# Layer 2 of a four-layer recurrent kernel: where the second sequence's queries, keys and values are projected

## The chip, the cores and the metric

The kernel runs on one core of one Trainium2 chip. The metric is the device time of one execution in microseconds (us); lower is better. One launch computes the whole model. The engines are TensorE (PE; its weight loads are shown as PEld), VectorE (DVE), ScalarE (ACT), GpSimd (POOL) and SyncE (SP, which issues DMAs). Each takes its own instructions in order and waits for the others by semaphores.

## The reference, cut to what matters

The model has four layers over 2 sequences of 1024 tokens with 128 channels. Each layer computes `x = x + s * silu(f)`, where `s` is a sequence mixer and `f` a feed-forward block, both from the layer-normed `x`. In layer 2 the block `f` begins with a softmax attention with 16 query heads of 8 channels in 4 groups that share keys and values:

```python
xr = rope(rms_norm(x, norm1_w))
Q = (xr @ Wq)      # 16 heads of 8
K = (xr @ Wk)      # 4 groups of 8
V = (xr @ Wv)      # 4 groups of 8
scores = einsum('bghsd,bgtd->bghst', Q, K) / sqrt(8)
attn = softmax(scores + causal_mask)
out = einsum('bghst,bgtd->bghsd', attn, V)
h = x + out.reshape(B, S, 128) @ Wo
```

A mixture of 8 experts (2 per token) follows on `h`, and beside it a linear attention gives `s`. The change concerns `Q`, `K` and `V` of the second sequence only.

## The kernel before

The tokens are 16 tiles of 128, 8 per sequence; four tiles make a group of 512 tokens (`G = 4`). `layer2` first normalises `x` (`Kern.normalise`), and then calls `Attention.prepare` once per sequence. For each group of 512 tokens, `prepare` scales the rows (`xw`, ACT), applies the rotation with six POOL instructions (`xr`, lines 1471 to 1476), and turns the result to channels by tokens (`xrT`: four transposes on PE, an eviction on ACT or DVE by turns). Then it projects: per group one product for the keys (`pk`), four for the queries (`pq`), and four small ones for the values (`pv`). Each fp32 product with 512 columns shows as two matmul instructions.

Keys and queries are evicted by `parts` (lines 1448 and 1449): ACT copies the product to `high`, rounded to fp32r, and DVE combines the product with `high`, so that every 8 channels are held as high and low parts. The values go through one DVE copy (line 1496) into `va`, which two POOL memsets prepare. In the preparation all eight PSUM banks belong to the pool `sn2`.

The attention is `softmax_attention`. Its PE order is written out by hand (`manual_schedule` for PE); the order on the other engines, and on PE outside this part, is made by a planner that runs the program against its own timeline and picks what is ready, earlier program order first. PSUM is divided anew: three banks with the tag `pm` (pool `sm2`), two pairs of banks for scores (`psc`, pool `sc2`), one for the output (`pat`, pool `so2`). The pool `pl` (`l2`) holds tiles of the loop in SBUF.

A step is one (sequence, query tile, key tile). There are 72 of them, sequence 0 first (36). For the softmax, the maxima of every query row are needed before its scores are exponentiated. They come from units: a score product into a `pm` bank (`pm<-kT,qT`; for the diagonal tile after a mask product, `pm<-ngeR,identR`), then a DVE reduction (line 1535) that frees the bank. When all units of a query tile are done, `largest` (lines 1543 to 1548) combines them and `turn` transposes the result (`pmt`, then `mT` on ACT). Four lead-in steps, -4 to -1, do only units, two masked and four plain ones each, so that the first maxima exist when step 0 begins. In steps from 0, PE also computes the scores (`psc`), ACT the exponentials (`pr`, line 291), and PE one step later the products with the values (`pat`).

`fill` is a list of (step, function): the functions are called at the head of the step, ahead of that step's masks, by `run(later.pop(s, ()))`. Before the change the list holds parts of the routing that come after half of the steps. Functions that the attention adds itself (`turn`, and the three parts of `close`) come behind those of `fill` in the same step.

In the lead-in, `take` hands out the units by their due steps:

```python
    for s in range(-4, 0):
        run(later.pop(s, ()))
        phase(take("masked", s, 99))
        phase(take("plain", s, 99))
        finish(s)
```

Of the kernel before, what the change touches and what calls it, by code (L numbers as in the profile page):

```python
# [10 lines left out]
F32 = mybir.dt.float32  # L11
# [8 lines left out]
P = 128  # L20
NB, SEQ = 2, 1024
# [3 lines left out]
G = 4  # L25
# [1057 lines left out]
def layer2(K, x, xn, xT, w, inp):  # L1083
    nc, tc, c = K.nc, K.tc, K.c
    four = [P, G, P]
    flat = lambda a: a.rearrange("p a b -> p (a b)")
    with ExitStack() as es:
# [9 lines left out]
        def norm(gs):  # L1097

            for i in range(gs[0] * G, gs[-1] * G + G):
                K.sumsq(keep, rs[:, i : i + 1], h[:, i, :])  # L1100
            at = slice(gs[0] * G, gs[-1] * G + G)
            K.powers(rs[:, at], rs[:, at], 1.0 / P, 1e-6)
            for g in gs:
                normed[g] = keep.tile(four, F32, name="hn", bufs=2)
                for j in range(G):
                    i = g * G + j
                    nc.vector.scalar_tensor_tensor(normed[g][:, j, :], h[:, i, :], rs[:, i : i + 1], w["n2"], ALU.mult, ALU.mult)
                nc.sync.dma_start(inp["lists"][0].rearrange("(i p) d -> p i d", p=P)[:, g * G : (g + 1) * G, :], normed[g])

        def hidden_columns(g, ps, tag):  # L1110
            pt = ps.tile(four, F32, name="tp", tag=tag)
            for j in range(G):
                nc.tensor.transpose(pt[:, j, :], normed[g][:, j, :], c["ident"])
            K.copy(hT[:, g * G * P : (g + 1) * G * P], flat(pt))

        with ExitStack() as e1:
            pf = e1.enter_context(tc.tile_pool(name="f2", bufs=1))
            K.phase("sqrt_and_others")
            seqs = [Attention(K, pf, xn, w, h, b) for b in range(NB)]
            ms = keep.tile([P, NT], F32, name="ms")  # L1120
            with tc.tile_pool(name="sn2", bufs=8, space=PSUM) as sn, tc.tile_pool(name="p2", bufs=1) as pp:

                n1 = w["n1"].rearrange("p (f two) -> p f two", two=2)
                turn = {}
                for n, a in (("cos", 0), ("sin", 0), ("cos", 1), ("sin", 1)):
                    turn[n, a] = pp.tile([P, TPB, 64], F32, name=f"{n}{a}")
                    nc.gpsimd.tensor_mul(turn[n, a], w[n], n1[:, :, a].unsqueeze(1).to_broadcast([P, TPB, 64]))
                K.normalise(pp, sn, x, xn, xT, None, ms)
                K.rsqrt(r2, ms, 1.0, 1e-5)
                for a in seqs:  # L1130
                    a.prepare(pp, sn, ms, turn)
            for rate, log in inp["rates"]:
                nc.scalar.activation(rate, log, AF.Exp)
            pl = e1.enter_context(tc.tile_pool(name="l2", bufs=1))
            for a in seqs:
                a.loop = pl
            K.phase("natural_log_exp_and_others")
            with tc.manual_schedule(engines={mybir.EngineType.PE}):
                with ExitStack() as e3:
                    sm = e3.enter_context(tc.tile_pool(name="sm2", bufs=3, space=PSUM))  # L1140
                    sc = e3.enter_context(tc.tile_pool(name="sc2", bufs=2, space=PSUM))
                    so = e3.enter_context(tc.tile_pool(name="so2", bufs=1, space=PSUM))

                    half = TPB * (TPB + 1) // 2
                    mid = TPB * (TPB + 1) - G * (G + 1) // 2
                    routed = [(half + 6, lambda: norm([0, 1])), (mid + 6, lambda: norm([3]))]
                    for g, s0 in ((0, half + 9), (1, half + 11), (3, mid + 9)):
                        routed.append((s0, lambda g=g: hidden_columns(g, sm, "pm")))
                        routed.append((s0 + 3, lambda g=g: K.group_logits(sm, "pm", lg, hT, g, w["wr"], w["br"], 8)))
                    softmax_attention(K, pf, sm, sc, so, seqs, routed)  # L1150
        with ExitStack() as e2:
            pa = e2.enter_context(tc.tile_pool(name="a2", bufs=1))
            pf = e2.enter_context(tc.tile_pool(name="m2", bufs=1))
# [6 lines left out]
            with tc.tile_pool(name="r2", bufs=1) as pr:  # L1160
                m1, m2, hot = K.top2(pr, lg, 8)
                d = Dispatch(K, pf, pr, sf, hot, 8, 2 * P, inp["lists"])
# [11 lines left out]
            for n in range(d.n):  # L1174
# [4 lines left out]
                t = pf.tile([P, inp["rows"].shape[2]], F32, name="tw", bufs=3)  # L1179
# [254 lines left out]
class Attention:  # L1434
# [16 lines left out]
    def prepare(self, pp, sc, ms, turn):  # L1451
        K, pf, xn, w, b = self.K, self.pf, self.xn, self.w, self.b
        nc, c = K.nc, K.c
        four = [P, G, P]
        xrT = pp.tile([P, SEQ], F32, name="xrT", bufs=2)
        rs = pp.tile([P, TPB], F32, name="ars", bufs=2)
        for g in range(TPB // G):
            tiles = range(b * TPB + g * G, b * TPB + g * G + G)
            gr = rs[:, g * G : (g + 1) * G]
            K.rsqrt(gr, ms[:, tiles.start : tiles.stop], 1.0, 1e-6)  # L1460
            xw = pp.tile(four, F32, name="xw", bufs=2)
            for j, i in enumerate(tiles):
                nc.scalar.activation(xw[:, j, :], xn[:, i, :], AF.Copy, scale=gr[:, j : j + 1])
            pair = xw.rearrange("p t (f two) -> p t f two", two=2)
            xe, xo = pair[:, :, :, 0], pair[:, :, :, 1]
            at = slice(g * G, g * G + G)
            cose, sine, coso, sino = (turn[n, a][:, at, :] for a in range(2) for n in ("cos", "sin"))
            xr = pp.tile(four, F32, name="xr", bufs=2)
            t2 = pp.tile([P, G, 64], F32, name="t2", bufs=2)
            t3 = pp.tile([P, G, 64], F32, name="t3", bufs=2)  # L1470
            nc.gpsimd.tensor_mul(xr[:, :, :64], xe, cose)
            nc.gpsimd.tensor_mul(t2, xo, sino)
            nc.gpsimd.tensor_sub(xr[:, :, :64], xr[:, :, :64], t2)
            nc.gpsimd.tensor_mul(xr[:, :, 64:], xe, sine)
            nc.gpsimd.tensor_mul(t3, xo, coso)
            nc.gpsimd.tensor_add(xr[:, :, 64:], xr[:, :, 64:], t3)
            K.to_feature_major(sc, lambda i: xr[:, i % G, :], xrT, g)
        self.qT = qT = pf.tile([P, 4, SEQ], F32R, name="qT", bufs=2)
        self.kT = kT = pf.tile([P, SEQ], F32R, name="kT", bufs=2)
        self.va = va = pf.tile([P, TPB, 4, 32], F32, name="va", bufs=2)  # L1480
        nc.gpsimd.memset(va, 0.0)
        nc.gpsimd.memset(va[:, :, :, 8], 1.0)
        for g in range(TPB // G):
            cols = slice(g * 512, (g + 1) * 512)
            pk = sc.tile([P, 512], F32, name="pk", tag="ps")
            K.mm(pk, w["wk"], xrT[:, cols])
            self.parts(pp, kT[:, cols], pk, w["klow"])
            for j in range(4):
                pq = sc.tile([P, 512], F32, name="pq", tag="ps")
                K.mm(pq, w["wq"][:, j, :], xrT[:, cols])  # L1490
                self.parts(pp, qT[:, j, cols], pq, w["qlow"])
            pv = sc.tile([P, G, 32], F32, name="pv", tag="ps")
            for j in range(G):
                i = g * G + j
                K.mm(pv[:, j, :], xrT[:, i * P : (i + 1) * P], w["wv"])
            nc.vector.tensor_copy(va[:, g * G : (g + 1) * G, :, :8], pv.rearrange("p t (g d) -> p t g d", d=8))

    def banks(self, sb):

# [393 lines left out]
def build(tc, io, packs):  # L1893
    nc = tc.nc
    with ExitStack() as ctx:
# [25 lines left out]
        with tc.tile_pool(name="const2", bufs=1) as pool0:  # L1921
            views.update((n, load(pool0, n)) for n in ("l1", "l2"))
            layer1(K, x, xn, xT, views["l1"], {"rows": io["rows1"], "lists": pair, **{n: io[n] for n in ("sw1", "sw3", "sw2")}})
            rates = {d: later.tile([P, 2], F32, name=d + "rate") for d in "fb"}
            layer2(K, x, xn, xT, views["l2"], {"rows": io["rows2"], "lists": pair, "rates": [(rates[d], views["l3"][d + "A_log"]) for d in "fb"]})
# [18 lines left out]
```

## Time and profile before

| | us |
|---|---|
| median of 3 runs | 1352.11 |
| lowest and highest | 1345.19, 1353.02 |
| the profiled execution's own time | 1337.11 |
| span of its trace | 1335.3 |
| PE busy (6697 matmuls) | 1145.4 (86%) |
| DVE busy (2260) | 873.4 (65%) |
| ACT busy (919) | 506.2 (38%) |
| POOL busy (386) | 389.0 (29%) |
| mean granted TensorE clock | 0.905 |

Times in the text are from the start of the span. Layer 2's preparation runs from about 444 to 495.7 us: normalisation and rotation first, sequence 0's projection from 470.6 to 482.8, sequence 1's transposes to 484.0 and its projection from 484.2. The attention follows to about 810 us. The granted clock is the share of full speed that the throttle gave TensorE; it takes the values 0.50 and 1.00, in windows of 3.41 us. "Busy" for PE is from the modelled ends of pipelined matmuls, so a busy PE is not one at its peak. Where a line ends in [time <-engine tile line], it says how long the engine sat idle before it, and what it waited for.

### The profile page before, as it was taken

The page shows a single profiled execution, that of the slowest core. Times are in us where ns is not written, and L with a number is a line of the kernel's source. Part 1 is how long each engine was busy: PE and PEld are TensorE (multiplying, and loading weights), DVE is VectorE, ACT ScalarE, POOL GpSimd, SP SyncE. Part 2 cuts the span into 40 slices and gives each one's busy share as a digit, 9 for nine tenths or more (in the row PEclk, how much of TensorE's full clock was granted, in tenths as well). Part 3 has the DMA queues.
Part 4 walks back from the last instruction along what each step waited for, and adds up shares of the span by engine and source line. Part 5 has one row for each costly group of instructions (what it writes and reads, how often), then busy time and mean ns, then how long its engine had stood idle before and what let it go on. Part 6 is the DMA issues. An engine that isn't in the chain of part 4 may idle for free. (4 is left out here: it accounts for less than half of the span.)

```text
span 1335.3 us, 18604 instructions
## 1 busy us (share of the span) xinstructions
PE 1145.4 (86%) x6697; PEld 773.0 (58%) x6697; DVE 873.4 (65%) x2260; ACT 506.2 (38%) x919; POOL 389.0 (29%) x386
## 2 busy tenths in 40 slices
PE   5599987899998288899999994899999288999996
PEld 2267665888996145454445343677778254554555
DVE  7944368947757965768888537787765582353447
ACT  4633335123222241435555773144243244422221
POOL 0073530057542520000000000344674130634430
PEclk9799986899999585969999997799999668999998
DMA  2000003046352000000000000243445301222101
GB/s 91 1 0 1 1 15 126 4 149 180 117 142 79 0 1 0 1 0 1 1 1 17 1 9 8 97 132 106 125 128 160 109 39 42 41 55 57 47 17 32
DMA packets 37803, 71.26 MB, mean 53 GB/s; under 512 B 5275, under 2 KB 22176, under 8 KB 37328
## 3 DMA queue, kind: packets, MB, share of 16 engines
q1 hardware_dynamic: 31408, 55.09, 13.7%
q0 software_dynamic: 5440, 9.79, 3.0%
q10 hardware_dynamic: 864, 5.20, 1.1%
q8 instruction: 53, 0.87, 0.3%
q14 instruction: 38, 0.31, 0.1%
HBM read 62.58 MB, written 8.85 MB: 53 GB/s over the span
## 5 line engine op out<-in xcount | busy, mean ns | idle before, releaser
L1535 DVE TENSOR_REDUCE mx<-pm 128x1 f32<-128x512 f32 (+3 forms) x304 | 185.4, 656 | 76.5 <-PE pm L319 72.2
L1305 POOL DMA_INDIRECT xb<-xs,dfrom x85 | 84.7, 997 | 491.7 <-PE psum L319 348.3
L291 ACT ACTIVATE pr<-psc 128x1024 f32<-128x1024 f32 x144 | 139.6, 1021 | 101.8 <-PE psc L319 69.5
L319 PE MATMUL pm<-kT,qT 32*128 32x128 f32 (+3 forms) x576 | 110.3, 370 | 7.5 <-DVE mx L1535 6.8
L319 PEld LDWEIGHTS pm<-kT,qT 32*128 32x128 f32 x576 | 68.1, 206 | 78.9 <-DVE mx L1535 52.7
L1315 POOL DMA_INDIRECT ys<-yb,dto x85 | 87.1, 1024 | 80.0 <-DVE yb L1202 49.4
L319 PE MATMUL p<-xbT,tw 128*128 128x256 f32 x368 | 99.8, 387 | 3.7 <-ACT sg L1195 2.6
L319 PE MATMUL pat<-pr,va 128*32 128x512 f32 x576 | 80.8, 633 | 0.9 <-DVE ao L316 0.9
L325 PE MATMUL tp<-w_c,xn 128*128 128x128 f32 x64 | 20.2, 413 | 71.2 <-DVE xn L369 45.1
L1195 ACT ACTIVATE sg<-p,tw 128x256 f32<-128x256 f32 x92 | 41.1, 472 | 90.8 <-PE p L319 86.5
L319 PEld LDWEIGHTS p<-xbT,tw 128*128 128x128 f32 x368 | 63.1, 193 | 14.6 <-ACT sg L1195 4.5
L319 PE MATMUL psc<-qT,kT 32*128 32x512 f32 x288 | 64.3, 492 | 3.8 <-ACT pr L291 3.8
L1196 DVE SCALAR_TENSOR_TENSOR hh<-p,tw,sg 128x256 f32<-128x256 f32 x92 | 42.5, 479 | 32.3 <-ACT sg L1195 23.2
L1874 POOL TENSOR_TENSOR hT<-hT,gb 128x512 f32<-128x512 f32 x32 | 41.3, 1294 | 72.0 <-DVE hT L1872 67.9
L319 PEld LDWEIGHTS po<-tw,hh 128*128 128x128 f32 x368 | 54.7, 193 | 9.4 <-issue 3.6
L1872 DVE TENSOR_TENSOR hT<-hT,put 128x512 f32<-128x512 f32 x36 | 24.5, 685 | 54.5 <-PE put L319 53.1
L325 PEld LDWEIGHTS tp<-w_c,xn 128*128 128x128 f32 x64 | 11.8, 191 | 78.8 <-ACT lnrs L291 45.7
L319 PE MATMUL po<-tw,hh 128*128 128x128 f32 x368 | 56.6, 277 | 0.5 <-DVE hh L1196 0.4
L319 PE MATMUL psc<-mT,onesR 32*128 32x512 f32 x288 | 54.7, 419 | 0.0
L291 ACT ACTIVATE hT<-pgt 128x512 f32<-128x512 f32 x36 | 21.4, 597 | 72.4 <-PE pgt L319 70.0
L605 POOL TENSOR_TENSOR uda<-w_c,vdA 128x512 f32<-128x512 f32 x28 | 28.6, 1041 | 62.1 <-PE pe L319 36.9
L646 DVE TENSOR_TENSOR uxdt<-pt,vdt 128x512 f32<-128x512 f32 x16 | 10.4, 684 | 47.9 <-PE pt L644 47.8
(523 smaller groups left out, 2756.4 us busy)
## 6 DMA issues: line engine op xcount, KB each, us to landing
tw<-in_rows SPq DMA_DIRECT2D x23, 836.0 KB, 4.5
tw<-in_rows SPq DMA_DIRECT2D x39, 384.0 KB, 3.3
gb<-gt SPq DMA_DIRECT2D x32, 256.0 KB, 4.1
yt<-ys SPq DMA_DIRECT2D x16, 256.0 KB, 3.2
w_l<-in_l ACTq DMA_DIRECT2D x1, 1890.0 KB, 11.6
w_e<-in_e SPq DMA_DIRECT2D x1, 1536.0 KB, 8.5
xb<-xs,dfrom POOLq DMA_INDIRECT x85, 2.8
ys<-yb,dto POOLq DMA_INDIRECT x85, 2.3
```

Source lines behind the costliest of these rows:

```text
L291: op = self.nc.scalar.activation(out, in_, func, **kw)
L319: self.nc.tensor.matmul(out, lhsT=lhsT, rhs=rhs, start=start, stop=stop)
L325: self.nc.tensor.transpose(pt[:, j, :], src(g * G + j), self.c["ident"])
L605: pool.tensor_mul(da, upto.unsqueeze(1).unsqueeze(1).to_broadcast(lay), m["dA"][:, i0 + j : i0 + j + per, :].unsqueeze(3).to_broadcast(lay))
L646: nc.vector.tensor_mul(heads(xdt[:, k]), heads(pt), each(m["dt"], k))
L1195: nc.scalar.activation(sg, p1[:, k - k0, :], AF.Silu, bias=t[:, 1536 + k : 1537 + k])
L1196: nc.vector.scalar_tensor_tensor(hh[:, k, :], p2[:, k - k0, :], t[:, 1540 + k : 1541 + k], sg, ALU.add, ALU.mult)
L1305: self.K.nc.gpsimd.indirect_dma_start(dst, None, self.xs, bass.IndirectOffsetOnAxis(self.of_token[:, n : n + 1], 0))
L1315: d = self.K.nc.gpsimd.indirect_dma_start(self.ys, bass.IndirectOffsetOnAxis(self.to[:, n : n + 1], 0), src, None, bounds_check=2 * T - 1, ...
L1535: nc.vector.tensor_reduce(mx[:, starts.index(a), g, j : j + k], tile[0][:, : k * m].rearrange("p (j m) -> p j m", m=m), AX.X, ALU.max)
L1872: nc.vector.tensor_mul(hT, hT, put)
L1874: nc.gpsimd.tensor_mul(hT, hT, gb[k // 2][:, k % 2, :])
```

## The change

`prepare` is cut in two. What is left of it scales, rotates and transposes, and keeps `xrT` in the longer-lived pool `pf`. The new method `project` allocates `qT`, `kT` and `va`, and returns twelve functions: for each of the two groups of 512 tokens one for the keys, four for the queries, one for the values. Sequence 0's are all called in the preparation, now after both sequences were prepared. Sequence 1's are put into the attention's list: numbers 0 to 7 in pairs at the heads of the lead-in steps -4 to -1, numbers 8 to 11 at the heads of steps 0 to 3. There they take their PSUM banks from the three with the tag `pm`, and `high` from the loop's pool.

```diff
--- before.py
+++ after.py
@@ -1129,6 +1129,8 @@
                 K.rsqrt(r2, ms, 1.0, 1e-5)
                 for a in seqs:
                     a.prepare(pp, sn, ms, turn)
+                for part in seqs[0].project(pp, sn, "ps"):
+                    part()
             for rate, log in inp["rates"]:
                 nc.scalar.activation(rate, log, AF.Exp)
             pl = e1.enter_context(tc.tile_pool(name="l2", bufs=1))
@@ -1147,6 +1149,8 @@
                     for g, s0 in ((0, half + 9), (1, half + 11), (3, mid + 9)):
                         routed.append((s0, lambda g=g: hidden_columns(g, sm, "pm")))
                         routed.append((s0 + 3, lambda g=g: K.group_logits(sm, "pm", lg, hT, g, w["wr"], w["br"], 8)))
+                    second = seqs[1].project(pl, sm, "pm")
+                    routed += [(n // 2 - 4 if n < 8 else n - 8, part) for n, part in enumerate(second)]
                     softmax_attention(K, pf, sm, sc, so, seqs, routed)
         with ExitStack() as e2:
             pa = e2.enter_context(tc.tile_pool(name="a2", bufs=1))
@@ -1452,7 +1456,7 @@
         K, pf, xn, w, b = self.K, self.pf, self.xn, self.w, self.b
         nc, c = K.nc, K.c
         four = [P, G, P]
-        xrT = pp.tile([P, SEQ], F32, name="xrT", bufs=2)
+        self.xrT = xrT = pf.tile([P, SEQ], F32, name="xrT", bufs=2)
         rs = pp.tile([P, TPB], F32, name="ars", bufs=2)
         for g in range(TPB // G):
             tiles = range(b * TPB + g * G, b * TPB + g * G + G)
@@ -1475,25 +1479,36 @@
             nc.gpsimd.tensor_mul(t3, xo, coso)
             nc.gpsimd.tensor_add(xr[:, :, 64:], xr[:, :, 64:], t3)
             K.to_feature_major(sc, lambda i: xr[:, i % G, :], xrT, g)
+
+    def project(self, pp, sc, tag):
+        K, pf, w = self.K, self.pf, self.w
+        nc, xrT = K.nc, self.xrT
         self.qT = qT = pf.tile([P, 4, SEQ], F32R, name="qT", bufs=2)
         self.kT = kT = pf.tile([P, SEQ], F32R, name="kT", bufs=2)
         self.va = va = pf.tile([P, TPB, 4, 32], F32, name="va", bufs=2)
         nc.gpsimd.memset(va, 0.0)
         nc.gpsimd.memset(va[:, :, :, 8], 1.0)
+        out = []
         for g in range(TPB // G):
             cols = slice(g * 512, (g + 1) * 512)
-            pk = sc.tile([P, 512], F32, name="pk", tag="ps")
-            K.mm(pk, w["wk"], xrT[:, cols])
-            self.parts(pp, kT[:, cols], pk, w["klow"])
+
+            def columns(name, weight, dst, low, cols=cols):
+                ps = sc.tile([P, 512], F32, name=name, tag=tag)
+                K.mm(ps, weight, xrT[:, cols])
+                self.parts(pp, dst[:, cols], ps, low)
+
+            def rows(g=g):
+                pv = sc.tile([P, G, 32], F32, name="pv", tag=tag)
+                for j in range(G):
+                    i = g * G + j
+                    K.mm(pv[:, j, :], xrT[:, i * P : (i + 1) * P], w["wv"])
+                nc.vector.tensor_copy(va[:, g * G : (g + 1) * G, :, :8], pv.rearrange("p t (g d) -> p t g d", d=8))
+
+            out.append(lambda columns=columns: columns("pk", w["wk"], kT, w["klow"]))
             for j in range(4):
-                pq = sc.tile([P, 512], F32, name="pq", tag="ps")
-                K.mm(pq, w["wq"][:, j, :], xrT[:, cols])
-                self.parts(pp, qT[:, j, cols], pq, w["qlow"])
-            pv = sc.tile([P, G, 32], F32, name="pv", tag="ps")
-            for j in range(G):
-                i = g * G + j
-                K.mm(pv[:, j, :], xrT[:, i * P : (i + 1) * P], w["wv"])
-            nc.vector.tensor_copy(va[:, g * G : (g + 1) * G, :, :8], pv.rearrange("p t (g d) -> p t g d", d=8))
+                out.append(lambda j=j, columns=columns: columns("pq", w["wq"][:, j, :], qT[:, j, :], w["qlow"]))
+            out.append(rows)
+        return out
 
     def banks(self, sb):
```

## The prediction

> **What bounds the kernel here.** I read the shares of the engines first, then the chain that ended last, then tables by stage. The chain can be followed back only to 1062.8 us, which is after layer 2's attention, so it says nothing of the changed stage. A microsecond there still reaches the end, because layer 2's dispatch and its experts need the attention's output for all tokens. So I took the busy time per stage. The columns are the stretch, its length, then busy time with counts of PE, PEld, DVE, ACT and POOL, then the granted TensorE clock, the DMA share and GB/s.
>
> ```profile
> 470.60:484.20 13.60, 13.37 (x44) 7.21 (x44) 8.06 (x13) 7.58 (x15) 4.89 (x7) 0.86 0.01 1
> 484.20:495.70 11.50, 10.55 (x36) 5.69 (x37) 8.52 (x15) 5.86 (x10) 0.19 (x1) 1.00 0.00 1
> 495.70:501.10 5.40, 3.87 (x26) 2.92 (x26) 3.22 (x7) 0.00 (x0) 0.15 (x2) 0.75 0.00 0
> 501.10:506.80 5.70, 4.32 (x19) 2.70 (x18) 3.89 (x9) 0.00 (x0) 0.00 (x0) 0.50 0.00 0
> 506.80:513.50 6.70, 5.64 (x23) 3.86 (x23) 4.69 (x8) 0.00 (x0) 0.00 (x0) 0.50 0.00 0
> 513.50:519.70 6.20, 4.82 (x20) 3.12 (x20) 3.55 (x10) 0.59 (x1) 0.00 (x0) 0.50 0.00 0
> 519.70:525.20 5.50, 5.15 (x28) 3.10 (x28) 2.27 (x5) 2.06 (x3) 0.00 (x0) 0.77 0.01 3
> 525.20:531.90 6.70, 6.07 (x30) 2.64 (x30) 3.77 (x10) 2.99 (x4) 0.00 (x0) 0.54 0.00 0
> 531.90:538.90 7.00, 6.57 (x38) 4.06 (x38) 3.21 (x7) 2.46 (x3) 0.00 (x0) 0.71 0.00 0
> 538.90:545.30 6.40, 4.78 (x35) 2.43 (x35) 5.61 (x14) 2.20 (x4) 0.00 (x0) 1.00 0.00 0
> ```
>
> The first row projects sequence 0, the second sequence 1, the next four are the lead-in steps -4 to -1, the last four are steps 0 to 3. The second row is almost pure PE work at full clock. In the lead-in, PE is busy 18.65 of 24.0 us although its clock is about half, and DVE 15.35: the two take turns. So no stretch holds a large idle PE into which 10.55 us of PE work would vanish.
>
> **What is removed.** The stretch 484.2 to 495.7 before the first mask product: 11.5 us. The sequence-1 transposes (482.8 to 484.0) stay before the attention, and one last eviction of that stage (a copy of 0.28 to 0.69 us) must still free its bank, so I count 11.2 us gained.
>
> **What is added at the same places.** Twelve pieces: per 512 tokens, one for keys, four for queries, one for values. Two go to the head of each of steps -4 to -1, one to the head of each of steps 0 to 3. The price of a piece comes from the rows of the removed stretch:
>
> ```profile
> 485.18 3.17 PE L319 MATMUL pq<-xrT,w_l 128*128 128x512 f32 x7
> ...
> 486.23 0.59 ACT L1448 CAST high<-pq 128x512 fp32r<-128x512 f32 x1 [0.27 <-PE pq L319]
> ...
> 486.85 1.61 DVE L1449 SCALAR_TENSOR_TENSOR qT<-high,w_l,pq 128x512 fp32r<-128x512 f32 x2
> ```
>
> A piece is two matmul instructions 0.43 us apart, so 0.86 us of PE at full clock. Under the clock of 0.50 before 474.5 us, the same weight loads start 0.85 us apart, so 1.7 us. From the matmul's start at 485.18 to the end of the first DVE instruction (486.85 + 0.75 = 487.60) the piece holds its PSUM bank for 2.4 us, or 3.3 us cold. A values piece is eight small instructions, 0.97 us warm (estimated 1.9 cold, doubled), and a 0.28 us copy. The sum of the second row is 10 x 0.86 + 2 x 0.97 = 10.5 us, which agrees with its 10.55.
>
> Now one lead-in step as it is, the one from 501.11:
>
> ```profile
> 501.11 1.22 PE L319 MATMUL pm<-ngeR,identR 128*128 128x512 f32 x2
> ...
> 502.26 1.11 PE L319 MATMUL pm<-kT,qT 32*128 32x128 f32 x9
> 503.41 1.29 DVE L1535 TENSOR_REDUCE mx<-pm 128x4 f32<-128x512 f32 x2 [1.50 <-PE pm L319]
> ...
> 506.84 1.27 PE L319 MATMUL pm<-ngeR,identR 128*128 128x512 f32 x2
> ```
>
> Two mask products, the scores, reductions on DVE that free banks, four plain products, the next step. The new pieces stand in front of the masks in PE's fixed order and take banks from the same three. **Cold step:** the two pieces take 3.4 us of PE; the first one's bank is free at 3.3, so the second mask does not wait. The step shifts by 3.4. **Full-clock step:** the pieces take 1.72, the first mask takes the third bank, and the second mask waits until the first piece's bank is back at about 2.45. Its scores can start at 2.8 where they started at 0.65, a shift of 2.1. Queued behind this waiting mask on PE are all score products of the step, and DVE's reductions wait for them. DVE gets 2 x 0.75 us and ACT 2 x 0.59 us per step; ACT is idle there, DVE was idle 1.8 to 2.7 us per step, so these hide. If they did not, they would cost up to 6 us over the lead-in.
>
> Sum of the lead-in: step -4 starts right behind dense work at full clock, 2.1; steps -3 and -1 cold, 3.4 each; step -2 has a values piece, 1.7 + 1.9 = 3.6. That is 12.5 us. All warm it would be 4 x 2.1 = 8.4, and the old work of steps -3 to -1 would shrink as well. I bound that shrinking by half their PE time (7.4 us) above and nothing below, and use 3.5, since DVE alone needs 12.1 of those 18.6 us.
>
> Steps 0 to 3: three query pieces and one values piece cost PE between 3 x 0.86 + 0.97 = 3.6 us and 3 x 1.7 + 1.9 = 7.0 us. PE idles 3.0 us in these steps; at best all of that absorbs, at worst none. I take 4.5.
>
> **The clock** decides between the two ends. Rows by the throttle's own windows of 3.41 us (stretch, length, PE busy and count, clock, DMA share, GB/s):
>
> ```profile
> 494.96:498.37 3.41, 1.73 (x12) 1.00 0.00 0
> 498.37:501.79 3.42, 2.83 (x16) 0.50 0.00 0
> ...
> 512.03:515.44 3.41, 3.41 (x17) 0.50 0.00 0
> 515.44:518.85 3.41, 2.04 (x7) 0.50 0.00 0
> 518.85:522.27 3.42, 3.40 (x10) 0.50 0.02 5
> 522.27:525.68 3.41, 3.06 (x23) 1.00 0.00 0
> 525.68:529.09 3.41, 3.41 (x23) 0.50 0.00 0
> ```
>
> A window that is half idle halves the next one (498.37). A full one raises it (522.27), but not always: 512.03 to 515.44 is full and the next stays at 0.50. A new cold step opens with pieces 3.4, masks 1.15 and scores 1.1 us, 5.7 us without a gap. A window lies wholly inside that in (5.7 - 3.4) / 3.4 = two steps of three, and then one window or so runs at full clock before the waits on DVE end it. So I take back 1.5 us of the 12.5 and use **11.0**.
>
> [...]
>
> **Sum.** -11.2 + 11.0 + 4.5 = +4.3 us on the profiled execution, whose own time is 1337.1 us (span 1335.3). That execution is 15 us under the median of the timed runs, 1352.1, so I add the difference to the median: **1356 us**. Within 1% is 13.5 us either way, about what a measurement of this kernel can tell from no change.
>
> **Rivals.**
> *The clock stays up* (chance 0.20). Lead-in 8.4 - 3.5, steps 0 to 3 at 3.6, and the old work of steps 0 to 2, 19.2 us at clocks of 0.54 to 0.77, about 3 us shorter: -11.2 + 4.9 + 3.6 - 3 = -5.7, 1346 us. For it: the full windows counted above. Against: 494.96, where the same lead-in loses the clock at once.
>
> *The banks starve* (chance 0.14), the slow side. If, at the head of a step, only one of the three banks is free, a second piece waits for the first piece's DVE end. A pair then costs 2 x 3.3 = 6.6 instead of 3.4, four times 3.2 more, and each single piece its full 3.3 instead of about 1.2, four times 2.1 more: 21 us, so +25 and 1377 us. It passes 1% once the eight lead-in pieces wait over 1.15 us each (13.5 - 4.3 = 9.2). Against: at 501.11 and 506.84 both masks ran back to back, so two banks were free.
>
> *The saving doesn't come* (chance 0.10). The change also puts sequence 1's rotation before sequence 0's projection in program order. If the planner puts its transposes ahead on PE, PE sits from 470.6 until POOL's last result at 476.7, 6 us: +10, 1362 us. For it: program order is the planner's preference. Against: now PE takes rotated transposes at 466.36 between those of the normalisation, so it chooses by readiness.
>
> The forecast itself gets 0.56: 1356, on its own between 1350 and 1364 by the bounds of the terms.
>
> **Range and chances.** [...] From 560 to 600 us PE gets 229 instructions done at clock 0.75, from 600 to 640 us 299 at 0.99, so such a stretch can move some 8 us either way without any cause in the pieces. The range takes in the fast rival with part of that, and the slow rival up to its half: 1342 to 1370. Slower by over 1%: starvation 0.14, plus 0.04 from the others with a bad clock. Faster by over 1%: 0.04, from the fast rival with a good clock. Within: 0.78.
>
> **What would show it.** The first mask product should start some 2 us after sequence 1's first piece instead of 11.5, and the first exp (523.73) should move by -11.2 + 11 + about 1, so hardly. Lead-in steps should be near 8 us instead of 6. If step lengths grow by only 1 us with a clock near 1.0, the fast rival holds; if PE's waits for DVE in the lead-in (8.0 us of weight loads behind the reductions) double, the banks starve; if PE idles before the first sequence-0 projection past 471 us, the planner spent the saving. Wrong also if the time moves after 810 us, where nothing was edited.

## The result, and the profile after

| | before | after |
|---|---|---|
| median of 21 runs each, us | 1349.54 | 1358.87 |
| lowest and highest, us | 1335.57, 1359.67 | 1349.34, 1363.93 |
| ratio after/before, 95% interval | | 1.0085 (1.0065 to 1.0105) |
| the profiled execution's own time, us | 1337.11 | 1363.49 |

The change makes the kernel slower by 0.85%, some 11.5 us (8.8 to 14.2). Ratios here and below leave out executions more than 1.5% above the fastest of the same kernel, here six of before's 21 and none of the changed kernel's, so 0.85% is more than the 9.3 us between the medians would give. The two profiled executions differ by 26.4 us, because that of before lies near its fastest run and that of after near its slowest. 8.47 of the 26.4 us are there before the edit: the first rotated transpose starts at 466.36 us before and at 474.83 after, and up to it PE and ACT execute their instructions in the same order in both. So I compare lengths from that transpose on, not absolute times.

The same table by step as in the prediction (stretch, length, busy time of PE, PEld, DVE, ACT and POOL, granted clock, DMA share, GB/s) for the changed kernel, cut at the first instruction of each step: four lead-in steps, then steps 0 to 3.

```profile
498.02:505.48 7.46, 5.40 (x31) 3.28 (x31) 4.57 (x7) 1.17 (x2) 0.00 (x0) 0.92 0.01 3
505.48:514.30 8.82, 7.13 (x23) 3.57 (x23) 5.28 (x11) 1.17 (x2) 0.00 (x0) 0.68 0.00 0
514.30:523.31 9.01, 7.95 (x28) 5.16 (x29) 4.93 (x9) 0.59 (x1) 0.00 (x0) 0.51 0.00 0
523.31:531.99 8.68, 7.52 (x23) 3.77 (x22) 4.87 (x11) 1.76 (x3) 0.00 (x0) 0.70 0.00 0
531.99:541.07 9.08, 8.94 (x34) 5.55 (x33) 4.22 (x10) 2.21 (x4) 0.00 (x0) 0.50 0.01 2
541.07:549.91 8.84, 8.00 (x34) 3.41 (x33) 4.43 (x11) 4.02 (x5) 0.00 (x0) 0.50 0.00 0
549.91:561.03 11.12, 10.34 (x40) 5.14 (x40) 3.98 (x8) 3.11 (x4) 0.00 (x0) 0.50 0.00 0
561.03:570.51 9.48, 8.70 (x43) 5.23 (x43) 5.60 (x14) 1.94 (x2) 0.00 (x0) 0.50 0.00 0
```

Cut in the same way, the steps of before last 5.40, 5.74, 5.78 and 6.25 us, and then 6.33, 6.72, 7.02 and 5.80. (The prediction's rows end steps -2 and -1 behind the transposes `pmt`, which open the next step.) The lead-in grew from 23.17 to 33.97 us, +10.8, and steps 0 to 3 from 25.87 to 38.52, +12.65. In these last four rows PE is nearly always busy and the clock stays at 0.50, where steps 0 to 3 of before had 0.54 to 1.00. The lead-in of before in one row, from its first instruction to the first score mask (`psc<-nleR`), for comparison with the rows further below:

```profile
495.70:520.71 25.01, 19.65 (x86) 13.42 (x87) 15.35 (x31) 1.17 (x2) 0.15 (x2) 0.55 0.00 1
```

The timeline of PE in the changed kernel (start, duration, engine, line, operation, tiles, shape, count; in brackets the idle time in front and what ended it), from the second four rotated transposes to the first instructions of the lead-in:

```profile
476.43 1.06 PE L325 MATMUL tp<-w_c,xr 128*128 128x128 f32 x4
483.82 1.11 PE L325 MATMUL tp<-w_c,xr 128*128 128x128 f32 x4 [6.33 <-POOL xr L1480]
485.18 1.11 PE L325 MATMUL tp<-w_c,xr 128*128 128x128 f32 x4 [0.25 <-POOL xr L1480]
486.09 1.56 PE L319 MATMUL pk<-xrT,w_l 128*128 128x512 f32 x2
...
498.02 1.10 PE L319 MATMUL pk<-xrT,w_l 128*128 128x512 f32 x2 [0.94 <-DVE va L1505]
498.96 1.02 PE L319 MATMUL pq<-xrT,w_l 128*128 128x512 f32 x2
499.42 0.80 PE L319 MATMUL pm<-ngeR,identR 128*128 128x512 f32 x1
500.63 0.49 PE L319 MATMUL pm<-ngeR,identR 128*128 128x512 f32 x1 [0.42 <-DVE kT L1453]
```

And in the kernel before, from the first rotated transposes to the first instruction of the lead-in:

```profile
466.36 1.09 PE L325 MATMUL tp<-w_c,xr 128*128 128x128 f32 x4 [0.48 <-issue]
467.24 0.96 PE L325 MATMUL tp<-w_c,xn 128*128 128x128 f32 x3
...
470.61 2.07 PE L319 MATMUL pk<-xrT,w_l 128*128 128x512 f32 x2 [1.55 <-ACT xrT L314]
...
495.70 0.71 PE L319 MATMUL pm<-ngeR,identR 128*128 128x512 f32 x2 [0.94 <-DVE va L1496]
```

The second line of the changed kernel is the main finding. After sequence 0's transposes, PE waits 6.33 us for POOL, which is still rotating sequence 1, and only then turns sequence 1's tiles and begins sequence 0's first projection. Before, that projection began 4.25 us after the first rotated transpose; now it begins 11.26 us after it. So the lead-in starts only 6.15 us earlier than before (23.19 us after the first transpose where it was 29.34), not the 11.2 of the removed stretch. Its last lines show the banks at work: the second mask of step -4 waits 0.42 us until the first piece's eviction has freed its bank.

From 810 us (the first product after the attention) to the end, nothing was edited and little moved: 524.6 us before, 527.9 after, where two more profiles of before (below) have 528.1 and 523.7.

### The profile page after: what moved, and what is told of

The parts are those of the page before. It is cut to its first block, busy times and chain, and to the rows that moved or that the text cites. A ratio compares the mean times of both kernels' runs of the same rounds, so it can differ in the third digit from the quotient of the medians.

```text
span 1361.7 us, 18587 instructions
## 1 busy us (share of the span) xinstructions
PE 1160.0 (85%) x6697; PEld 780.7 (57%) x6697; DVE 871.2 (64%) x2260; ACT 506.3 (37%) x919; POOL 390.7 (29%) x386
## 5 line engine op out<-in xcount | busy, mean ns | idle before, releaser
L319 PE MATMUL po<-tw,hh 128*128 128x128 f32 x368 | 57.5, 281 | 0.5 <-DVE hh L1200 0.4
L605 POOL TENSOR_TENSOR uda<-w_c,vdA 128x512 f32<-128x512 f32 x28 | 28.6, 1041 | 62.8 <-PE pe L319 38.1
```

The lines of the kernel that those rows point to most:

```text
L319: self.nc.tensor.matmul(out, lhsT=lhsT, rhs=rhs, start=start, stop=stop)
L605: pool.tensor_mul(da, upto.unsqueeze(1).unsqueeze(1).to_broadcast(lay), m["dA"][:, i0 + j : i0 + j + per, :].unsqueeze(3).to_broadcast(lay))
```

## Experiments

**Theory P (planner).** Calling `prepare` for both sequences first makes the planner place sequence 1's transposes ahead of sequence 0's projection on PE. That costs 5 to 6 us, about half of what the removed stretch gives. **Rival.** The order is harmless, and all of the loss comes from the pieces inside the attention. Two kernels separate these. `e1_order_kept` has the pieces as in the change, but the old program order:

```diff
-                for a in seqs:
-                    a.prepare(pp, sn, ms, turn)
+                seqs[0].prepare(pp, sn, ms, turn)
                 for part in seqs[0].project(pp, sn, "ps"):
                     part()
+                seqs[1].prepare(pp, sn, ms, turn)
```

> The change, but sequence 0 is projected in the preparation before sequence 1 is prepared, as in the kernel before; the twelve pieces stay where the change put them. Theory A (the planner's order costs 5.1 us, lead-in and steps the rest): about 6 us slower than before, ratio 1.0045, and PE starts sequence 0's first key product without waiting for POOL's rotation of sequence 1. Theory B (the pieces alone cost everything, the wait for POOL is made good later): ratio 1.0085 as with the whole change.

Measured: 1349.32 us, ratio 1.0023 (0.9989 to 1.0056), about 3 us over before, where theory P expected 6. The timeline of PE in this kernel, the first projection of sequence 0 and the first piece:

```profile
475.34 2.07 PE L319 MATMUL pk<-xrT,w_l 128*128 128x512 f32 x2 [1.57 <-ACT xrT L314]
...
489.41 1.10 PE L319 MATMUL pk<-xrT,w_l 128*128 128x512 f32 x2 [0.88 <-DVE xrT L316]
```

The first rotated transpose is at 471.10 here, so the projection begins 4.24 us after it, as before the change, and the lead-in 18.31 us after it: 11.03 us gained, against 6.15 in the change. The lead-in steps last 7.37, 9.15, 9.15 and 8.75 us (+11.25) and steps 0 to 3 last 8.81, 5.98, 6.83 and 6.60 (+2.35). The sum -11.0 + 11.25 + 2.35 = +2.6 us stands beside the measured +3; what the clock does behind step 3 in this one profile is not in it.

`e2_order_only` is the opposite: both sequences are prepared first, as in the change, and both are projected there, with no pieces in the attention.

```diff
-                for part in seqs[0].project(pp, sn, "ps"):
-                    part()
+                for a in seqs:
+                    for part in a.project(pp, sn, "ps"):
+                        part()
...
-                    second = seqs[1].project(pl, sm, "pm")
-                    routed += [(n // 2 - 4 if n < 8 else n - 8, part) for n, part in enumerate(second)]
```

> Both sequences are prepared first, then both are projected in the preparation; no piece is in the attention. Theory A: PE waits about 6 us for POOL ahead of sequence 0's projection and gets back 1 us, so about 5 us slower than before, ratio 1.004. Theory B: ratio 1.000, the wait is covered.

Measured: 1349.39 us, 1.0031 (0.9994 to 1.0068). The timeline of its PE:

```profile
485.96 1.12 PE L325 MATMUL tp<-w_c,xr 128*128 128x128 f32 x4 [6.30 <-POOL xr L1479]
488.23 1.92 PE L319 MATMUL pk<-xrT,w_l 128*128 128x512 f32 x2
```

The wait of 6.3 us comes with the order alone, and the lead-in begins 5.08 us later than before, measured from the first rotated transpose (34.42 against 29.34). In the time of the whole kernel this alone (some 4 us) is not told from nothing by its interval. But e1 and the changed kernel, which differ in the order alone, differ in their ratios too (1.0023 and 1.0085, intervals that do not meet). So theory P holds for what stands ahead of the projection and for the late start of the lead-in; how many of its 5 us reach the whole time is less sure.

**The changed kernel again.** +12.65 us in steps 0 to 3 was far over the 4.5 predicted, and PE had its half clock throughout. Either the pieces do that, or this one execution drew a bad clock. `a2_change_again` and `a3_change_again` are the changed kernel, unaltered.

> The changed kernel once more, for its profile. If the stretch of half clock over steps 0 to 3 (51 us in the first profile, 12.7 us longer than before) belongs to the change, steps 0 to 3 take 35 us or more again. If it is where the work fell on the clock's windows, they take 27 to 33 us, as the 28.2 us of the run with the order kept. PE's wait for POOL of 6.3 us ahead of sequence 0's projection returns in any case.

> The same once more: steps 0 to 3 at 35 us or more if the half clock there belongs to the change, 27 to 33 us if it does not; the 6.3 us wait in any case; the lead-in between 34 and 38 us.

Measured: 1355.56 and 1363.74 us. The timeline of PE in the first of them: the wait, the head of step 0, and the head of step 4.

```profile
484.90 1.12 PE L325 MATMUL tp<-w_c,xr 128*128 128x128 f32 x4 [6.32 <-POOL xr L1480]
...
532.22 2.08 PE L319 MATMUL pq<-xrT,w_l 128*128 128x512 f32 x2
...
561.67 0.33 PE L1625 MATMUL patT<-w_c,at 128*128 128x128 f32 x1 [1.35 <-DVE mx L1550]
```

From the second line to the third are 29.45 us, and 29.45 again in the other repeat: +3.6 over before, not +12.65. So 9 us of the first profile, in these steps, belong to that execution alone. But both repeats lose clock later. Their stretch from the 7th to the 19th group of value products (roughly steps 8 to 19) takes 57.54 us, where the first profile of the change has 49.68 at a clock of 1.00. In the first repeat:

```profile
577.73:635.27 57.54, 54.25 (x358) 27.35 (x357) 42.11 (x82) 26.68 (x37) 0.00 (x0) 0.82 0.00 1
```

The lead-in takes 32.5 and 32.7 us, a little less than was expected of these runs, and the wait on POOL returns each time (6.32 and 6.30).

**Place or banks?** From its first instruction to the first score mask, the lead-in takes 24.66 to 25.01 us in all profiles without pieces there, and 38.51 in e1. Theory B: the pieces take `pm` banks that the units need. Rival: PE is given more work at the head of a step, where nothing else runs, and the bank does not matter. `e7_heads_other_banks` is e1 with the eight lead-in pieces in the score pairs, which nobody uses before step 0.

```diff
-                ps = sc.tile([P, 512], F32, name=name, tag=tag)
+                used.append(name)
+                sc, tag = lead if len(used) <= 8 else rest
+                ps = sc.tile([P, 512], F32, name=name, tag=tag)
...
-                    second = seqs[1].project(pl, sm, "pm")
+                    second = seqs[1].project(pl, (sc, "ps"), (sm, "pm"))
```

> Preparation in the order of before; the pieces at the places of the change, but the eight of the lead-in take banks of the score pool, which the lead-in does not use otherwise. Bank theory (the three shared banks are what makes a piece at a step's head cost 3 us a pair): the stretch from the first lead-in instruction to the first score mask falls from 38.5 to below 30 us. Place theory (in front of the masks PE has nothing to wait for, so a piece there is only added, wherever its bank is): it stays at 36 to 38 us, only the 0.4 us waits for the piece's bank go; ratio near 1.002.

Measured: 1346.62 us, 1.0019 (0.9990 to 1.0047). The lead-in in one row, to the first score mask:

```profile
492.11:527.29 35.18, 29.41 (x111) 16.98 (x111) 21.39 (x38) 5.86 (x10) 0.00 (x0) 0.71 0.00 1
```

Against e1 the banks are worth 3.3 us of the 13.5; the rest stays when they are free. These are single profiles: with the same pieces in the shared banks, the three profiles of the change take 36.6 to 38.1 us, so the banks may be worth as little as 1.4. At the head of a step the place costs most.

`e4_gaps` therefore moves the pieces off the heads. All twelve are in the lead-in, three a step, behind the masked units, behind three plain ones and at the end, so that each stands where PE would wait for a DVE reduction. Their banks are the score pairs.

```diff
-                    second = seqs[1].project(pl, sm, "pm")
-                    routed += [(n // 2 - 4 if n < 8 else n - 8, part) for n, part in enumerate(second)]
-                    softmax_attention(K, pf, sm, sc, so, seqs, routed)
+                    second = seqs[1].project(pl, sc, "ps")
+                    softmax_attention(K, pf, sm, sc, so, seqs, routed, second)
...
         phase(take("masked", s, 99))
-        phase(take("plain", s, 99))
+        pieces.pop(0)()
+        plain = take("plain", s, 99)
+        phase(plain[:3])
+        pieces.pop(0)()
+        phase(plain[3:])
+        pieces.pop(0)()
```

> Preparation in the order of before; all twelve pieces in the lead-in, three a step, placed behind the masked units, behind the first three plain units and at the step's end, in banks of the score pool that the lead-in does not use. Theory A (PE's own time is what counts, full clock within reach): PE's 5.4 us of waiting in the lead-in is filled, the lead-in grows by 5 us instead of 10.8, steps 0 to 3 not at all: -11.2 + 5, 6 us faster than before, ratio 0.9955. Theory C (the half clock sets the price): each piece costs 1.7 us, 20 us less 5.4 of waiting, so 3 to 4 us slower than before, ratio 1.003.

Measured: 1342.55 us, 0.9951 (0.9917 to 0.9985), faster than before. The lead-in in one row:

```profile
491.33:517.27 25.94, 24.21 (x122) 13.00 (x123) 21.98 (x41) 6.67 (x12) 0.00 (x0) 1.00 0.00 1
```

Some 10.5 us of PE work at full clock were added, and the stretch is 0.9 us longer than before (25.01); the ratio says the whole kernel is 6.6 us faster (2.0 to 11.2), the terms -10.7 + 0.9 = -9.8. PE is now busy 24.21 of 25.94 us, but at a clock of 1.00 where it was 0.55. The timeline of PE shows a step of it:

```profile
498.57 1.13 PE L319 MATMUL pq<-xrT,w_l 128*128 128x512 f32 x2
499.62 0.40 PE L319 MATMUL pm<-kT,qT 32*128 32x256 f32 x2
500.24 0.49 PE L319 MATMUL pm<-kT,qT 32*128 32x256 f32 x4 [0.22 <-DVE mx L1549]
500.67 1.13 PE L319 MATMUL pq<-xrT,w_l 128*128 128x512 f32 x2
501.85 0.50 PE L319 MATMUL pm<-kT,qT 32*128 32x256 f32 x2
```

A piece of 1.13 us runs while DVE reduces, and the score product behind it waits 0.22 us, where such waits last 0.46 to 0.79 us in steps -3 to -1 of the kernel before.

`e8_gaps_shared_banks` is e4 with the pieces in the three `pm` banks again.

```diff
-                    second = seqs[1].project(pl, sc, "ps")
+                    second = seqs[1].project(pl, sm, "pm")
```

> The twelve pieces in the gaps of the lead-in, three a step, but in the three shared banks. Bank theory: the same stretch is 35 us or more, since each piece keeps a bank for 2.4 us and the units wait. Place theory: it stays below 29 us, near the 25.9 with the other banks, ratio 0.995 to 0.998.

Measured: 1354.91 us, 1.0047 (1.0003 to 1.0091). Its lead-in in one row:

```profile
489.14:533.33 44.19, 38.74 (x122) 20.27 (x123) 23.15 (x41) 7.03 (x12) 0.00 (x0) 0.61 0.00 1
```

And a step of it in the timeline of PE:

```profile
499.78 1.13 PE L319 MATMUL pq<-xrT,w_l 128*128 128x512 f32 x2
500.83 0.73 PE L319 MATMUL pm<-kT,qT 32*128 32x256 f32 x2
502.36 0.58 PE L319 MATMUL pm<-kT,qT 32*128 32x256 f32 x4 [0.80 <-DVE qT L1452]
503.53 2.08 PE L319 MATMUL pq<-xrT,w_l 128*128 128x512 f32 x2 [0.58 <-DVE mx L1549]
```

44.2 us against 25.9 with the same work in the same places: here the bank decides. A score product waits 0.80 us for the eviction of a piece (`qT`), the next piece then comes late and at half clock (2.08), and the clock sinks to 0.61. So neither theory holds alone. At the heads the place costs most; in the gaps the banks do.

With nothing but the banks changed, the clock of the lead-in is 1.00 in e4 and 0.61 in e8; in e8 it comes back for one window only (499.2 to 502.6 us) and then stays at 0.50 to the end of the lead-in.

**Is the gain the place or the clock?** `e5_late_steps` puts one piece at the head of each of steps 8 to 19, in `pm` banks and with the order kept, where PE is busy 46 of 50 us and runs at full clock in six of the eleven profiles that have no pieces there.

```diff
-                    routed += [(n // 2 - 4 if n < 8 else n - 8, part) for n, part in enumerate(second)]
+                    routed += [(n + 8, part) for n, part in enumerate(second)]
```

> Preparation in the order of before; the twelve pieces one a step at the heads of steps 8 to 19, where the clock was 1.0 in most windows. Theory A: 0.86 us of PE each at full clock, 10.5 us for 11.2 saved, ratio 0.9995, with the lead-in as in the kernel before. Bank theory: each piece holds up the step by its 2.4 us in the bank, 29 us, so 18 us slower, ratio 1.013. Theory C (clock): if the clock falls to 0.5 in these steps, 20 us for 11.2, ratio 1.007.

Measured: 1338.97 us, 0.9937 (0.9908 to 0.9967), a larger gain than expected. The stretch from the 7th to the 19th group of value products holds these twelve steps; its row in this kernel:

```profile
556.08:615.63 59.55, 56.88 (x395) 28.45 (x394) 49.64 (x94) 32.51 (x47) 0.00 (x0) 1.00 0.00 1
```

Without the pieces the stretch takes 49.7 us at full clock (e2 and e4), so twelve pieces cost 9.87 us there, 0.82 each: their full price of 0.86, hardly hidden. The preparation gives 10.8 back. The terms thus say about -1 us, the ratio says -8.5 (-4.4 to -12.4). One candidate for the rest was the stretch of half clock at 580 to 600 us in the profile of before, which e5 does not have: 57.54 us there against 49.7. So the kernel before was profiled twice more.

> The kernel before, unchanged, profiled a second time; it tells where the whole gain of the late pieces (8.5 us in the median, about 1 us by the terms) can have come from. If the half clock at 580 to 600 us of the first profile belongs to the kernel, the steps from the 7th to the 19th group of value products take 57.5 us again, the late pieces buy back those 7.9 us of lost clock, and the gain is explained. If it is a draw of the single execution, the steps take about 49.7 us, and that explanation falls for at least part of the executions. The stretch from the first lead-in instruction to the first score mask: 25 us in both cases.

> The same once more: 57.5 us for the steps from the 7th to the 19th group of value products if the lost clock is regular, about 49.7 us if it is drawn in each execution; the lead-in stretch 25 us in both cases.

Measured: own times 1341.38 and 1335.42 us. The same stretch in the first profile of before:

```profile
562.39:619.93 57.54, 54.29 (x359) 27.61 (x358) 42.12 (x83) 26.71 (x37) 0.00 (x0) 0.82 0.00 1
```

and in the second:

```profile
568.67:618.38 49.71, 45.80 (x358) 23.27 (x357) 41.83 (x83) 26.54 (x37) 0.00 (x0) 1.00 0.00 1
```

The third has 49.66; the lead-in takes 24.9 and 24.7 us, as was expected. So this loss of 7.9 us comes in some executions only, and the steady explanation falls. Of the eleven profiles without pieces in these steps, six have 49.7 us, four 57.5 (the first of before, both repeats of the change, e7) and e1 55.15; the three with pieces there (e5, e9, e10) keep a clock of 1.00. What the runs do show is that e5's times spread less: 1334.15 to 1340.88 us in 12 runs, and 1333.86 to 1359.95 in the 35 of before beside them. The lowest times are nearly equal, as the terms demand; the high ones are gone. That fits draws of the clock that before loses more often than e5 does, but the longest executions of before were not profiled, and it stays open.

`e9_idle_products` asks for the clock directly: e5, and in addition twelve products that nobody reads, at e4's places in the lead-in, in the score pairs. It adds work to the reference's and leaves nothing out.

```diff
+                    def idle():
+                        K.mm(sc.tile([P, 512], F32, name="pz", tag="ps"), w["wk"], seqs[1].xrT[:, :512])
+
-                    softmax_attention(K, pf, sm, sc, so, seqs, routed)
+                    softmax_attention(K, pf, sm, sc, so, seqs, routed, [idle] * 12)
```

> The pieces one a step in steps 8 to 19, and in the lead-in's gaps twelve more products of the same size whose results nobody reads: work is added, none left out. Clock theory (the half clock is what the lead-in's 24.7 us are made of, and full-width work in the gaps keeps the clock up): the stretch does not grow by the 10.3 us of PE that is added, it stays between 22 and 26 us at a clock near 1.0, ratio as without them, 0.994. Theory without the clock: PE's waits of 5.4 us are filled and the rest is added, 30 us, ratio 0.998.

Measured: 1338.79 us, 0.9962 (0.9931 to 0.9993). The lead-in in one row, in e5:

```profile
488.35:513.06 24.71, 19.20 (x86) 13.02 (x87) 15.19 (x29) 1.17 (x2) 0.00 (x0) 0.57 0.00 1
```

and in e9:

```profile
489.04:512.63 23.59, 23.45 (x110) 11.74 (x111) 15.30 (x29) 0.90 (x2) 0.00 (x0) 1.00 0.00 1
```

With 12 products more (24 instructions, 10.3 us at full clock) the stretch is 1.1 us shorter, since the clock goes from 0.57 to 1.00. So the lead-in has room for about that much PE work, and it costs no time there if it stands in PE's waits with banks of its own. In the whole time e9 is not told from e5.

`e10_split` puts the two places together: eight pieces in the gaps, two a step, and four at the heads of steps 8 to 11.

```diff
-                    softmax_attention(K, pf, sm, sc, so, seqs, routed, second)
+                    routed += [(n, part) for n, part in enumerate(second[8:], 8)]
+                    softmax_attention(K, pf, sm, sc, so, seqs, routed, second[:8])
...
         phase(plain[3:])
-        pieces.pop(0)()
```

> Eight pieces in the lead-in's gaps, two a step, in banks of the score pool, and four at the heads of steps 8 to 11. If both places are nearly free: at or below the better of the two alone, ratio 0.993. If the lead-in needs three a step to keep its clock: the stretch to the first score mask goes to 30 us and the ratio to 0.998.

Measured: 1334.77 us, 0.9928 (0.9894 to 0.9963), the lowest median of all. It beats the kernel before by some 10 us. Its lead-in takes 25.10 us at a clock of 0.86, so two pieces a step do not hold the full clock as three do in e4 (1.00), and yet it does not grow to 30. Against e5 and e4 its interval does not decide.

## Why the prediction was right in its range and wrong in its cause

The forecast was +4.3 us and 1356, the result +11.5 us (8.8 to 14.2) and 1358.87. The sign and the range held. That 1356 lies so near 1358.87 is in part luck: it was added to a median of three runs, 1352.11, where 21 runs gave 1349.54, and the difference itself was missed by 7 us. The way there did not hold, because a rival that I gave 0.10 is what happened, and its +10 us is the nearer number.

**The step that failed** is "so I count 11.2 us gained", with the argument against the third rival that the planner "chooses by readiness". The lead-in began only 6.15, 5.5 and 5.0 us earlier in the three profiles of the change. PE sits 6.3 us in front of sequence 1's transposes, as that rival had it ("6 us: +10"). With the order kept, the same edit gains 11.03 (e1). The sign that I had named for it, PE idle ahead of the first sequence-0 projection, is there too (6.33 us). The transposes that I had seen at 466.36 do stand ahead of three transposes of the normalisation, which come earlier in the program: in that place later work went first. From this one place I concluded that the planner would not let PE wait for earlier work while later work is ready on the chip. In the changed kernel it did. It judges readiness by its own timeline, and I did not ask where that puts POOL's rotation. Why it placed the transposes there is not shown by any run.

**The lead-in**, forecast +11.0: measured +10.8, +9.3 and +9.5 in the change and +11.25 in e1. By step: +2.06, +3.08, +3.23 and +2.43, where I had 2.1, 3.4, 3.6 and 3.4, less 1.5 for windows that rise. (One row that I showed spoke against counting on full windows, and I passed over it: 522.27 to 525.68 is busy for 3.06 of 3.41 us, and the next window has 0.50. Nor do the readings that I took from single rows hold as rules over the trace of before, cut from 27 us on into 382 such windows, each wholly at 0.50 or at 1.00: after the eight at 1.00 in which PE was busy for 40 to 60%, the next had 0.50 three times, and after the 32 at 0.50 in which it was busy for 90% or more, the next had 1.00 in 20 cases.) The full-clock step came out as worked: the shift was 2.06, and the second mask waited 0.42 us for the first piece's bank.

**Steps 0 to 3**, forecast +4.5, from 3.6 to 7.0 us of PE work of which up to 3.0 might hide: +3.6 in both repeats and +2.35 in e1. The +12.65 of the first profile is a draw of the clock, outside my bounds, which assumed that the old work of these steps would not change its price. The 8 us that I allowed for a stretch at a lower clock elsewhere is about what the runs show (57.54 against 49.7).

**Banks starve** (0.14): small at the heads, 1.4 to 3.3 us by e7, since two banks are free there as argued. It is real where the pieces meet the reductions (e8, 44.19 us against 25.94 in e4). **The clock stays up** (0.20): not at the heads, where the lead-in of the change had 0.67. But the lead-in can be held at 1.00 (e4, e9), and my statement that no stretch holds a large idle PE into which 10.55 us would vanish was wrong: at a clock of 0.55 PE looked busy 19.65 of 25.01 us, and at full clock almost 10.5 us more fitted into 25.94.

The sum as measured, by the two repeats: -5.3 (mean of 5.5 and 5.0) + 9.4 + 3.6 = +7.7 us; by the first profile, -6.15 + 10.8 + 12.65 = +17.3. That is +10.9 on the mean of the three. The whole way from the first rotated transpose to the first product after the attention lasts 359.0, 349.9 and 354.4 us in the three profiles of the change and 344.3, 341.5 and 339.4 in those of before, +12.7 on the mean. So the preparation and the attention alone can account for the measured 9 to 11.5 us, but with draws of the clock of 8 and 9 us in them. How often each kernel makes such a draw is not shown: three profiles of each are too few. A stretch of 20 us or more at a clock of 0.50 between steps 0 and 20 stands in all five profiles with pieces at the heads of the lead-in (the change, e1, e7) and in two of the nine others (the first of before, e10). So the pieces at the heads may also make it more frequent; no run decides that.

## What to carry to other kernels

Where a planner orders an engine's work, moving a call in the program moves more than the call: look up what now stands ahead of ready work, and what it waits for. Work moved into a phase in which an engine and its consumer take turns was nearly free here only inside that engine's waits and with buffers that the phase did not need (e4: some 10.5 us of PE work, the stretch 0.9 us longer); at the head of a step (e7: eight pieces, 10.2 us longer), or in its buffers (e8: 19.2 us longer), it cost its full price or more. A busy share at half clock hid room here (e5: busy 19.20 of 24.71 us at 0.57; e9: 10.3 us more of PE work in 23.59 us at 1.00), and a single profile contained a draw of the clock nearly as large as the change (7.9 and 9 us against 11.5), so read two or three of the same program before a term of a sum is called wrong.

## What the runs showed of the hardware that was not expected

More PE work made a stretch shorter: 10.3 us of products that nobody reads, and 24.71 became 23.59 us, with the clock going from 0.57 to 1.00.

Nearly full work did not bring the clock back in the changed kernel's first profile. Here is its row between two idle gaps of PE, each of 0.64 us:

```profile
549.91:560.39 10.48, 10.34 (x40) 5.14 (x40) 3.37 (x6) 3.11 (x4) 0.00 (x0) 0.50 0.00 0
```

As far as the modelled ends of the products tell, PE is busy for 10.34 of 10.48 us, and the clock stays at 0.50 to the end; 20 of the 40 products are of shape 32\*128 and eight of 128\*32. Short waits did not keep the clock up either: in e5's lead-in the longest wait of PE was 0.78 us, and the clock was 0.57.

The same stretch of the same program took 38.52, 29.45 and 29.45 us (steps 0 to 3 in the three profiles of the change), and 57.54, 49.71 and 49.66 (steps 8 to 19 in the three of before).

One thing stays unexplained. In the three profiles of the change and in e2 the first rotated transpose starts at 474.8 to 477.0 us, in the three of before at 466.4 to 470.7, and in the seven with the order kept at 469.8 to 472.9, though nothing is edited ahead of it. The difference begins in layer 1. A timeline of PE in the change's first repeat,

```profile
218.52 3.85 PE L319 MATMUL plg<-w_l,xT 128*128 128x8 f32 x18
```

and in the second profile of before:

```profile
219.02 2.07 PE L319 MATMUL plg<-w_l,xT 128*128 128x8 f32 x18
```

The same 18 products run at half clock in all four profiles with the new order (the change's three and e2), but also in e7, where the order is kept; in the other nine they take 2.07 to 2.46 us. Whether the change has a part in that or these are draws isn't settled, nor how much of the measured difference it holds.
